# Two rows W·a₁ and W·a₂ for a graph-attention layer: made on the engines in place of a trip through DRAM

## The chip, the core and the metric

The kernel runs on one core of one Trainium2 chip. A core has five engines with an instruction stream each: PE (matrix products), DVE (vector), ACT (scalar activations), POOL (GpSimd, which here mostly issues indirect transfers) and SP (which here only issues plain transfers). Sixteen DMA engines are shared by all queues of the core. The metric is the device time of one execution in microseconds, as the median of several runs.

## The reference, cut to what matters

Two layers work on x of 32 batches × 512 nodes × 512 features, with a sparse 512×512 adjacency matrix (about four edges for each node).

```python
h = relu(layernorm(x))
x = x + attention(h, adj)          # 8 heads of 64, scores masked by adj, then @ Wo + bo
h = relu(layernorm(x))
g = h @ W                          # layer 1
s1 = g @ a[:512];  s2 = g @ a[512:]
e = leaky_relu(s1[:, None] + s2[None, :], 0.2) * adj
x = x + elu(softmax(e) @ g + beta * g)
```

The sums s1 and s2 need no product h·W first: s1 = h·(W a₁) and s2 = h·(W a₂). So the kernel makes two vectors of 512 numbers once, W a₁ and W a₂, spreads each over all 128 partitions as the tiles `wa1_r` and `wa2_r`, and afterwards needs one dot product for each node and each of the two.

## The kernel before, in words

Each batch is cut into four tiles of 128 nodes. Stage a of a batch normalises x, turns it (transposes on PE), and makes queries, keys and values: queries by four products of 128×512 for each tile, keys and values for two tiles together by seven half products in Strassen's manner (`keys_and_values`, L851). They are written to tables in DRAM. Stage b gathers, tile by tile, the table rows of each edge's two ends (POOL, L959 and L986), multiplies and sums them (DVE, L1037 and L1041), weighs the values (ACT, L1051), adds up edges by products with a 0/1 matrix into `px` (L1017), divides (L1077), turns the result, multiplies by Wo, adds x, normalises again and stores the row hx for layer 1 (`layer0`, L1022). In it the two dot products with `wa2_r` and `wa1_r` stand at L1106 and L1110 (their trace line is L1102). Layer 1 of a batch runs in the stage b of the batch two later (LAG = 2). So batches 0 and 1 come first without any layer-1 work, and their gathers read smaller tables (`tkv`).

The order of the instructions on each engine is written out by a planner when the kernel is built (`Plan.order`, L118). Every operation has an engine, an estimated time, a due time called key, and the buffers it reads and writes. The planner steps through a simulated time and takes on each engine the ready operation with the lowest key. A ready operation with a late key is taken as soon as no other one is ready on its engine. The estimates only decide the order; on the chip each engine runs its list strictly in that order and waits for what an instruction needs. Each key of the main stages is 100 plus 20 for each tile that came before.

Of the start, what the change touches: `constants` (L349) lists small loads on SP with key 20, among them the columns `bq_c` and `bk_c`. These hold the two biases with one word for each partition and column, which are only read in `general_path`, the branch taken for inputs that the fast path can't treat. `dot_rows` (L690) makes the two rows. For g = 0 and 1: SP loads a₁ or a₂ to all partitions (L695), DVE multiplies it with the four 128-row blocks of W and sums (L699, four times), which leaves W·a as a 128×4 tile `wa[g]`; SP writes those 512 words to a DRAM row in the right order (L702), and when that has landed reads the row back to all partitions (L705). The keys are KD and KD + 10 with KD = 110.

The products with the matrix of ones that the change uses exist already in `edges` (L377): `turn` (L421) multiplies a diagonal matrix by a column, and a product with `onesP` adds over partitions, so that a column becomes a row on all partitions. PSUM banks for such results come from the ring `D` (six banks, taken in the order in which operations need one); the ring `w` has four 128×512 tiles.

Of the kernel before, what the change touches and what calls it, by code (L numbers as in the profile page):

```python
# [9 lines left out]
F32 = mybir.dt.float32  # L10
I32 = mybir.dt.int32
AF = mybir.ActivationFunctionType
ALU = mybir.AluOpType
# [6 lines left out]
P = 128  # L20
# [19 lines left out]
def product(nc, out, lhsT, rhs, start=True, stop=True):  # L40

    nc.tensor.matmul(out, lhsT, rhs, start=start, stop=stop)  # L42


def bcast_rows(ap, n):

    return bass.AP(tensor=ap.tensor, offset=ap.offset, ap=[[0, P], [1, n]])
# [17 lines left out]
class Plan:  # L65
# [14 lines left out]
    def buf(self, tag, name=""):  # L80
        return Buf(tag, name)

    def op(self, eng, us, key, fn, r=(), w=(), dma=0, form=128):
        def parts(xs):
            return [x if isinstance(x, tuple) else (x, None) for x in xs]

        r, w = parts(r), parts(w)
        o = Op(eng, us * self.PACE.get(eng, 1.0), key, fn, r, w, [], dma)
        o.form = form
        evict = eng in ("DVE", "ACT") and any(b.tag in self.free_order for b, _ in r + w)  # L90
        o.rank = key - self.FREE * evict
        for xs, write in ((r, False), (w, True)):
            for b, part in xs:
                for other, opart, owrite in b.log:
                    if (write or owrite) and other is not o and (
                        part is None or opart is None or part == opart
                    ):
                        o.before[other] = True
                b.log.append((o, part, write))
        for b in dict.fromkeys(b for b, _ in r + w):  # L100
            b.users += 1
            if b.first is None and b.tag in self.rings:
                b.first = o
                o.alloc.append(b)
            elif b.first is not None and b.first is not o:
                o.behind[b.first] = True
        self.ops.append(o)
        return o
# [110 lines left out]
def kernel(  # L219
# [23 lines left out]
    nc = tc.nc  # L243
    B, N, D = x.shape
    T = N // P
    C = D // P
# [4 lines left out]
    def ctile(shape, name, dt=F32):  # L251
        return const.tile(shape, dt, name=name, tag=name)
# [3 lines left out]
    ident = ctile([P, P], "ident")  # L256
    bq_c, bk_c = ctile([P, C], "bq_c"), ctile([P, C], "bk_c")
    beta_b = ctile([P, 1], "beta_b")
    flag = ctile([1, 1], "flag", I32)
# [4 lines left out]
    dram = fast.enter_context(tc.tile_pool(name="dram", bufs=1, space=bass.MemoryType.DRAM))  # L264

    def wtile(shape, name, dt=F32):
        return work.tile(shape, dt, name=name, tag=name)

    def ring(n, shape, name):
        return [wtile(shape, f"{name}{i}") for i in range(n)]  # L270
# [23 lines left out]
        "dn": ring(3, [P, 3, T], "dn"),  # L294
        "s1": ring(3, [P, T], "s1"),
        "cs": ring(LAG + 1, [P, C], "cs"),
        "row": [dram.tile([N], F32, name=f"row{i}", tag=f"row{i}") for i in range(2)],
        "tab": [dram.tile([N + DUMMY, ROW], F32, name=f"tab{i}", tag=f"tab{i}") for i in range(LAG + 2)],
        "tkv": [dram.tile([N + DUMMY, HO], F32, name=f"tkv{i}", tag=f"tkv{i}") for i in range(LAG)],
        "th": [dram.tile([N + DUMMY, HW_], F32, name=f"th{i}", tag=f"th{i}") for i in range(LAG)],  # L300
# [5 lines left out]
    buf, op = plan.buf, plan.op  # L306

    wt2, wt3, wt4 = (wtile([P, C // 2, D], n) for n in ("wt2", "wt3", "wt4"))
    one32, onesP = wtile([P, G], "one32"), wtile([P, P], "onesP")
    bq_r, bk_r, c_row = (wtile([P, D], n) for n in ("bq_r", "bk_r", "c_row"))  # L310
    wa1_r, wa2_r = wtile([P, D], "wa1_r"), wtile([P, D], "wa2_r")
# [3 lines left out]
    perm, posi = wtile([P, T], "perm", I32), wtile([P, T], "posi", I32)  # L315
    fin = wtile([P, T, 2], "fin")
    rmax = wtile([P, T, H], "rmax")
    dmax = wtile([P, 2, T], "dmax")
    bad = wtile([P, T], "bad")
    cap = wtile([P, 2, T], "cap")  # L320
# [4 lines left out]

    C_ = {n: buf(None, n) for n in (
        "wq", "wk", "wv", "wo", "w1", "rows", "c_row", "wa", "OH", "nzE", "idx", "qidx", "fin",
        "rmax", "dmax", "bad", "cap", "flag", "perm", "posi", "t1", "t2", "t3", "t4",
    )}

    def setup():
# [16 lines left out]

    def constants():  # L349

        def load(fn, dma=4096, w=()):
            op("SP", 0.1, 20.0, fn, w=w, dma=dma)

        for dst, src in ((bk_r, bk), (bq_r, bq)):
            load(lambda dst=dst, src=src: nc.sync.dma_start(dst, bcast_rows(src, D)), P * D * 4, [C_["rows"]])
        load(lambda: nc.sync.dma_start(beta_b, bcast_rows(beta, 1)))
        zero = rings["qe"][-1].rearrange("p a b -> p (a b)")
        for tag, n in (("tkv", D), ("qtab", QW), ("th", HW_), ("tab", ROW)):
            for tab in rings[tag]:
                for c0, c1 in ((0, D), (HO, ROW)) if tag == "tab" else ((0, n),):  # L360
                    m = 1 if tag == "qtab" else DUMMY
                    load(lambda tab=tab, c0=c0, c1=c1, m=m: nc.sync.dma_start(
                        tab[N:, c0:c1], zero[:m, : c1 - c0]))
        for dst, src in ((bq_c, bq), (bk_c, bk)):
            load(lambda dst=dst, src=src: nc.sync.dma_start(
                dst, bass.AP(tensor=src.tensor, offset=src.offset, ap=[[1, P], [P, C]]),
                allow_slow_non_contiguous=True))

# [313 lines left out]
        op("DVE", 0.7, 30.0, lambda: nc.vector.scalar_tensor_tensor(  # L684
            c_row, c_row, -1.0, p.ap, op0=ALU.add, op1=ALU.add), r=[p], w=[C_["c_row"]])

    KD = 110.0
    GL, ZL = 0.5, 0.2

    def dot_rows():  # L690
        wa = buf("s1", "wa"), buf("s1", "wa")
        for g in range(2):
            ar, scr, row = buf("w", "ar"), buf("w", "scr"), buf("row", "wrow")
            k = KD + 10 * g
            op("SP", 0.1, k, lambda g=g, ar=ar: nc.sync.dma_start(  # L695
                ar.ap, bass.AP(tensor=a.tensor, offset=a.offset + g * D, ap=[[0, P], [1, D]])),
               w=[ar], dma=P * D * 4)
            for c in range(C):
                op("DVE", 0.8, k, lambda g=g, c=c, ar=ar, scr=scr: nc.vector.tensor_tensor_reduce(  # L699
                    scr.ap, w1[:, c, :], ar.ap, 1.0, 0.0, op0=ALU.mult, op1=ALU.add,  # L700
                    accum_out=wa[g].ap[:, c : c + 1]), r=[C_["w1"], ar], w=[scr, wa[g]])
            op("SP", 0.1, k, lambda g=g, row=row: nc.sync.dma_start(  # L702
                row.ap.rearrange("(t p) -> p t", p=P), wa[g].ap, allow_slow_non_contiguous=True),
               r=[wa[g]], w=[row], dma=2048)
            op("SP", 0.1, k, lambda g=g, row=row: nc.sync.dma_start(  # L705
                (wa1_r, wa2_r)[g], row.ap.unsqueeze(0).to_broadcast([P, N])),
               r=[row], w=[(C_["wa"], g)], dma=P * D * 4)

# [572 lines left out]

    load_weights()
    constants()
    edges()
    stage_a(0)
    right_sums()
    value_row()
    dot_rows()  # L1290
    for b in range(B + LAG):
        if b + 1 < B:
# [213 lines left out]
```

## Time and profile before

| what | value |
|---|---|
| median of 3 runs | 2711.84 us (2710.35 to 2716.46) |
| the profiled execution | 2710.42 us, with a span of 2708.6 us in the trace |
| PE busy | 2652.9 us |
| DVE, ACT, POOL busy | 2058.6, 1925.6 and 1830.4 us |
| DMA | 789.56 MB, 291 GB/s over the span |
| packets under 512 B | 34627 of 237154 |

The page divides the span into 40 slices and gives for each the busy share of the engines, the clock granted to PE, the share of the DMA engines and the rate. A second kind of view gives the same for stretches that one names. The views of waits say how long an engine stood still and which event ended it. The timeline lists instructions of one engine in order of time with the idle time before them in brackets.

### The profile page before, as it was taken

Reading aid. Unit: us, or ns where it says so; the run is one execution under the profiler, and the core shown is the slowest. Engines: PE = TensorE matmul, PEld = TensorE weight load, DVE = VectorE, ACT = ScalarE, POOL = GpSimd, SP = SyncE. Lnnn points to the kernel's source line nnn. Section 1 sums busy time; section 2 is a strip of 40 time slices with the busy share of each in tenths; the row PEclk is TensorE's granted clock in tenths of the full one; section 3 lists DMA queues with packets and bytes.
Section 4 is the critical chain, followed back from the end, with each engine's and each line's share of the span. In section 5 each row is a group of like instructions: output and inputs, shape, how many; then the busy total and the mean of one; then the engine's idle time right before and its main releaser. Section 6 shows DMA issues by size and latency. Waiting matters only on the chain. (4 is left out here: it accounts for less than half of the span.)

```text
span 2708.6 us, 39840 instructions
## 1 busy us (share of the span) xinstructions
PE 2652.9 (98%) x10262; PEld 1215.4 (45%) x10262; DVE 2058.6 (76%) x5241; ACT 1925.6 (71%) x6181; POOL 1830.4 (68%) x1710
## 2 busy tenths in 40 slices
PE   9999999999999999999999999999999999999987
PEld 4434444444444444444444444444444444444433
DVE  7767777777877777777777777777777777777675
ACT  1557777687777777777777777777777777777672
POOL 2776766666766766766766766766766766766664
PEclk9999999999999999999999999999999999999999
DMA  5988888888888888888888888988888988988984
GB/s 181 261 283 318 302 304 300 288 303 309 302 297 302 300 297 311 294 290 313 300 303 304 304 290 301 313 300 300 309 291 300 311 299 296 314 294 288 304 260 123
DMA packets 237154, 789.56 MB, mean 291 GB/s; under 512 B 34627, under 2 KB 34627, under 8 KB 236918
## 3 DMA queue, kind: packets, MB, share of 16 engines
q0 software_dynamic: 156736, 644.99, 70.6%
q1 hardware_dynamic: 80182, 141.95, 14.1%
q8 instruction: 83, 1.36, 0.2%
q14 instruction: 153, 1.25, 0.1%
HBM read 617.36 MB, written 169.46 MB: 290 GB/s over the span
## 5 line engine op out<-in xcount | busy, mean ns | idle before, releaser
L1051 ACT ACTIVATE kv<-kv 128x64 f32<-128x64 f32 x4096 | 1012.0, 336 | 5.2
L986 POOL DMA_INDIRECT qe<-qtab,qidx x504 | 550.3, 1092 | 218.9 <-issue 111.0
L959 POOL DMA_INDIRECT kv<-tab,idx x480 | 509.4, 1061 | 164.9 <-issue 112.3
L42 PE MATMUL pd<-wq,hT 128*128 128x512 f32 x1024 | 465.2, 597 | 1.4 <-ACT hT L795 1.4
L42 PE MATMUL pd<-wo,oT 128*128 128x512 f32 x1032 | 464.4, 593 | 0.1
L42 PE MATMUL pd<-w,gT 128*128 128x512 f32 x992 | 447.8, 594 | 0.0
L773 POOL DMA_INDIRECT x<-in_x_dram,perm x252 | 356.2, 1414 | 85.3 <-issue 51.0
L1037 DVE TENSOR_TENSOR qe<-qe,kv 128x1024 f32<-128x1024 f32 x252 | 307.2, 1220 | 39.2 <-DMA qe<-qtab,qidx 30.7
L1041 DVE TENSOR_REDUCE s<-qe 128x16 f32<-128x1024 f32 x252 | 305.7, 1214 | 0.1
L42 PEld LDWEIGHTS pd<-wq,hT 128*128 128x128 f32 x1024 | 195.3, 192 | 244.1 <-issue 241.5
L42 PEld LDWEIGHTS pd<-wo,oT 128*128 128x128 f32 x1032 | 194.7, 190 | 239.5 <-issue 220.3
L42 PEld LDWEIGHTS pd<-w,gT 128*128 128x128 f32 x992 | 188.4, 191 | 239.3 <-issue 230.8
L760 POOL TENSOR_TENSOR mv<-mv,mhalf 128x1 f32<-128x1 f32 x256 | 170.4, 666 | 170.0 <-DVE mv L757 152.7
L778 POOL DMA_INDIRECT out_dram<-w,perm x128 | 157.7, 1232 | 158.6 <-DVE w L1253 113.6
L871 PE MATMUL pd<-wt,S 128*128 128x512 f32 x496 | 238.1, 602 | 3.8 <-DVE k L879 3.7
L871 PE MATMUL pd<-wk,hT 128*128 128x512 f32 x496 | 237.9, 603 | 3.7 <-ACT hT L795 3.4
L871 PE MATMUL pd<-wv,S 128*128 128x512 f32 x496 | 233.6, 593 | 4.0 <-DVE S L860 2.1
L1247 ACT ACTIVATE w<-pd,dn 128x512 f32<-128x512 f32 x128 | 87.7, 685 | 194.6 <-PE pd L42 194.5
L1094 DVE TENSOR_TENSOR x<-pd,x 128x512 f32<-128x512 f32 x128 | 88.0, 687 | 127.8 <-PE pd L42 113.1
L1102 DVE CUSTOM_DVE_ANT_0 w<-hx,wa_r 128x512 f32<-128x512 f32 x256 | 175.2, 684 | 12.0 <-ACT hx L767 11.5
L755 DVE BATCH_NORM_STATS2 st<-x 128x6 f32<-128x512 f32 x256 | 176.3, 689 | 3.5 <-DMA x<-in_x_dram 0.9
L740 PEld LDWEIGHTS pd<-ident,w 128*128 128x128 f32 x1152 | 133.1, 141 | 82.2 <-issue 37.4
(217 smaller groups left out, 3590.1 us busy)
## 6 DMA issues: line engine op xcount, KB each, us to landing
qtab<-q SPq DMA_DIRECT2D x124, 258.0 KB
tab<-hx SPq DMA_DIRECT2D x120, 260.0 KB
tab<-v SPq DMA_DIRECT2D x120, 260.0 KB
tab<-k SPq DMA_DIRECT2D x120, 256.0 KB
qe<-qtab,qidx POOLq DMA_INDIRECT x504, 6.6
kv<-tab,idx POOLq DMA_INDIRECT x480, 8.0
x<-in_x_dram,perm POOLq DMA_INDIRECT x252, 7.6
th<-hx SPq DMA_DIRECT2D x8, 260.0 KB
```

Of the source, the lines that this page charges most:

```text
L42: nc.tensor.matmul(out, lhsT, rhs, start=start, stop=stop)
L755: nc.vector.bn_stats(s6.ap, src.ap)
L760: op("POOL", 0.75, key, lambda: nc.gpsimd.tensor_tensor(mv.ap[:, t, 2:3], mv.ap[:, t, 2:3], mhalf[:, 0:1], op=ALU.pow), w=[(mv, t)])
L773: nc.gpsimd.indirect_dma_start(dst, None, rows, bass.IndirectOffsetOnAxis(ap=perm[:, t : t + 1], axis=0), **lim)
L778: nc.gpsimd.indirect_dma_start(rows, bass.IndirectOffsetOnAxis(ap=perm[:, t : t + 1], axis=0), src, None, **lim)
L871: nc.tensor.matmul(p.ap, lhs()[:, c, :], rhs[:, c, :], start=first and c == 0, stop=c == K2 - 1, skip_group_check=True)
L959: nc.gpsimd.indirect_dma_start(dst, None, tab.ap, bass.IndirectOffsetOnAxis(ap=idx[:, t, g : g + 1], axis=0), bounds_check=N + DUMMY - 1, ...
L986: op("POOL", 1.3, kb - 0.84 * S + 0.1 * g, lambda qs=qs, g=g, t=t: nc.gpsimd.indirect_dma_start(q_row(qs, g), None, s["qtab"].ap, bass.Ind ...
L1037: nc.vector.tensor_tensor(q, q, sl.ap[:, at, KO : KO + D], op=ALU.mult)
L1041: nc.vector.tensor_reduce(sb.ap[:, at, :], q.rearrange("p n (h f) -> p n h f", f=HD), axis=AX.X, op=ALU.add)
L1051: nc.scalar.activation(p[:, h, 0:HD], p[:, h, 0:HD], AF.Copy, scale=p[:, h, HD : HD + 1])
L1102: nc.vector.tensor_tensor_reduce(scr.ap, hx.ap[:, 1 : D + 1], row, 1.0, 0.0, op0=ALU.mult, op1=ALU.add, accum_out=dst)
```

## The change

The two rows no longer pass through DRAM. DVE multiplies a diagonal matrix of 128×(4·128) by the column tile `wa[g]`, PE multiplies the result by the matrix of ones into a bank of the ring `D`, and ACT copies the bank to `wa1_r` or `wa2_r`. The two DRAM buffers fall away. KD goes from 110 to 100, so the eight multiply-and-sum operations get earlier keys too. The loads of `bq_c` and `bk_c` get the key 1500 in place of 20, and a mark `late` as the thing they write, which makes them follow one another.

```diff
@@ rings @@
-        "row": [dram.tile([N], F32, name=f"row{i}", tag=f"row{i}") for i in range(2)],
@@ constants @@
-        def load(fn, dma=4096, w=()):
-            op("SP", 0.1, 20.0, fn, w=w, dma=dma)
+        def load(fn, dma=4096, w=(), key=20.0):
+            op("SP", 0.1, key, fn, w=w, dma=dma)
...
         for dst, src in ((bq_c, bq), (bk_c, bk)):
             load(lambda dst=dst, src=src: nc.sync.dma_start(
                 dst, bass.AP(tensor=src.tensor, offset=src.offset, ap=[[1, P], [P, C]]),
-                allow_slow_non_contiguous=True))
+                allow_slow_non_contiguous=True), key=1500.0, w=[C_["late"]])
@@ dot_rows @@
-    KD = 110.0
+    KD = 100.0
...
-            ar, scr, row = buf("w", "ar"), buf("w", "scr"), buf("row", "wrow")
+            ar, scr, p = buf("w", "ar"), buf("w", "scr"), buf("D", "pwa")
...
-            op("SP", 0.1, k, lambda g=g, row=row: nc.sync.dma_start(
-                row.ap.rearrange("(t p) -> p t", p=P), wa[g].ap, allow_slow_non_contiguous=True),
-               r=[wa[g]], w=[row], dma=2048)
-            op("SP", 0.1, k, lambda g=g, row=row: nc.sync.dma_start(
-                (wa1_r, wa2_r)[g], row.ap.unsqueeze(0).to_broadcast([P, N])),
-               r=[row], w=[(C_["wa"], g)], dma=P * D * 4)
+            op("DVE", 0.7, k, lambda g=g, scr=scr: nc.vector.tensor_tensor(
+                scr.ap.rearrange("p (c q) -> p c q", c=C), ident.unsqueeze(1).to_broadcast([P, C, P]),
+                wa[g].ap.unsqueeze(2).to_broadcast([P, C, P]), op=ALU.mult), r=[wa[g]], w=[scr])
+            op("PE", 0.86, k, lambda scr=scr, p=p: product(nc, p.ap, onesP, scr.ap), r=[scr], w=[p])
+            op("ACT", 0.6, k, lambda g=g, p=p: nc.scalar.copy((wa1_r, wa2_r)[g], p.ap), r=[p], w=[(C_["wa"], g)])
```

More of the change, by code (lines that the diff above doesn't have):

```diff
@@ L327 @@
         "wq", "wk", "wv", "wo", "w1", "rows", "c_row", "wa", "OH", "nzE", "idx", "qidx", "fin",
-        "rmax", "dmax", "bad", "cap", "flag", "perm", "posi", "t1", "t2", "t3", "t4",
+        "rmax", "dmax", "bad", "cap", "flag", "perm", "posi", "late", "t1", "t2", "t3", "t4",
     )}
```

## The prediction

> **What bounds the kernel now.** I read the page's first lines, then busy time by stretches of 100 us, then PE's waits, then the start in steps of 2 us, then single instructions of SP, POOL and PE.
>
> ```profile
> span 2708.6 us, 39840 instructions
> PE 2652.9 (98%) x10262; PEld 1215.4 (45%) x10262; DVE 2058.6 (76%) x5241; ACT 1925.6 (71%) x6181; POOL 1830.4 (68%) x1710
> ```
>
> PE is the bound: only 2708.6 - 2652.9 = 55.7 us of the span are without a product. So a change is worth what it does to these 55.7 us, plus products added or removed. Where they lie (columns: stretch, length, busy us of PE, its weight loads, DVE, ACT, POOL; clock granted; DMA share; rate):
>
> ```profile
> 100.00:200.00 100.00, 90.66 (x313) 39.91 (x312) 67.52 (x142) 58.53 (x199) 73.97 (x68) 0.98 0.93 278
> 200.00:300.00 100.00, 95.69 (x379) 42.82 (x378) 76.30 (x179) 72.37 (x242) 68.46 (x64) 0.98 0.84 291
> 500.00:600.00 100.00, 97.13 (x397) 44.59 (x396) 74.50 (x192) 78.72 (x260) 65.07 (x62) 1.00 0.85 295
> 900.00:1000.00 100.00, 100.00 (x370) 46.32 (x369) 77.93 (x200) 77.11 (x253) 73.85 (x68) 1.00 0.91 316
> 2600.00:2700.00 100.00, 86.98 (x362) 38.09 (x362) 65.93 (x219) 51.52 (x141) 54.50 (x53) 0.91 0.56 166
> ```
>
> The first 100 us lose 5.8, the next two hundred 9.3 and 4.3, single waits up to 900 us about 7, then nothing up to 2500, and the end loses 30. PE's waits from 100 to 240 us (us in total, times, longest):
>
> ```profile
> PE pd L871 <- DVE k L879: 3.4, 1, 3.4
> PE pd L740 <- DVE w L1077: 3.3, 2, 3.1
> PE pd L871 <- DVE S L860: 2.1, 1, 2.1
> PE pd L740 <- ACT x L767: 1.4, 1, 1.4
> PE pd L931 <- DVE mv L762: 1.3, 1, 1.3
> ```
>
> With two smaller ones it is 13.2 us. Beside it, in the windows of 2 us, stands the trace of the word-by-word writes: DMA engines busy, hardly a byte moved.
>
> ```profile
> 96.00:98.00 2.00, 2.00 (x6) 0.95 (x5) 1.21 (x4) 2.00 (x9) 1.67 (x3) 1.00 0.96 335
> 102.00:104.00 2.00, 2.00 (x6) 0.76 (x4) 2.00 (x6) 1.83 (x8) 1.66 (x2) 1.00 0.57 61
> 122.00:124.00 2.00, 0.63 (x4) 0.00 (x1) 1.90 (x6) 2.00 (x8) 1.57 (x1) 1.00 0.59 48
> ```
>
> The chain behind it, from the timelines of SP, POOL and PE: the row is written at 96.90 and read back at 108.43, after its landing; likewise 110.60 and 129.41. POOL stands still for late transfers, its square roots (L760) come late, DVE stops behind them, and PE behind DVE.
>
> ```profile
> 96.90 0.37 SPq L702 DMA_DIRECT2D row<-s  x1
> 108.43 0.32 SPq L705 DMA_DIRECT2D wa_r<-row  x1
> 129.41 0.32 SPq L705 DMA_DIRECT2D wa_r<-row  x1
> 125.81 1.01 POOL L986 DMA_INDIRECT qe<-qtab,qidx  x1 [2.03 <-DMA kv<-tkv,idx]
> 132.72 1.00 POOL L959 DMA_INDIRECT kv<-tkv,idx  x1 [1.13 <-DMA x<-in_x_dram,perm]
> 144.01 1.09 POOL L760 TENSOR_TENSOR mv<-mv,mhalf 128x1 f32<-128x1 f32 x2
> 146.10 3.45 PE L871 MATMUL pd<-wt,S 128*128 128x512 f32 x4 [3.38 <-DVE k L879]
> 221.15 0.76 PE L740 MATMUL pd<-ident,w 128*128 128x128 f32 x4 [3.06 <-DVE w L1077]
> ```
>
> In the instruction order each POOL transfer waits for the landing of the one eight transfers before it; so slow DMA becomes POOL waits. POOL has little to give: from 80 to 180 us it is busy 16 of every 20 us and loses 0.3 us at nearly each issue, except for 4.9 us of waits between 123.8 and 132.7.
>
> **What the change removes.** Two writes of 512 words, two reads of 256 KB, four SP issues. From 90 to 98 us DMA moves 326 GB/s on average; from 100 to 108 it moves 113 and from 120 to 124 it moves 44. That is 5.2 and 3.5 us of transfer time lost, 8.7 in all. SP's wait of 7.5 us (two) before L705 goes too; queued behind it were a key store and the mean rows of `tkv` (L942 at 129.82), which batch 1's first gather at 149.11 reads with some 19 us to spare: nothing gained there.
>
> A rule of the Trainium skill speaks against a gain: "DMA: Bandwidth & Descriptors", section "Anatomy of one DMA — SWDGE (gpsimd) path", prices a transfer at a nearly constant 2.0 us plus its bytes at 436 GB/s. By it (stated for POOL's path) write and read-back cost 2.0 and 2.6 us, all hidden since the first reader of `wa_r` starts at 141.06, and the sum would be a loss of the added products alone. The trace has 11.5 us from first write to read-back and 18.8 for the second, and the low rates above. I go by the trace.
>
> **What it adds.** PE: two products of 128x512 with ones; the same product at 25.97 is followed by the next at 26.83, so 2 x 0.86 = 1.7 us, on the bound, counted in full. DVE: two diagonals, at 0.69 for the same operation (L423); ACT: two bank copies at 0.59 (L1092's row). From 100 to 120 us these engines are busy 13.2 and 10.2 of 20; were that cover gone, it would be 1.4 and 1.2 us. Each product also holds one of the six banks until ACT's copy. No row shows what that costs: from 0 (below it nothing, since a held bank frees no one) to the 3.4 of the nearest wait of this kind, at 146, where a bank waited for L879; I take 0, because both products stand where PE had no wait before.
>
> New waits: PE's products wait for DVE's diagonals, with a `px` group and half products queued behind. By the walk below the diagonals are ready near 96 and 105, and PE arrives at 102.5 and 106: no stall. ACT waits for each product, with a relu of x and the weighing of `kv` tile 96 behind it; they are done near 104.5 and 113.6, and PE wants them at 116 and 118: covered, with some 5 us to spare.
>
> **What it moves.** The bias columns are not moved far back. In the new order the load of `bq_c` stands where it stood and that of `bk_c` two places later, behind the fourth x tile and `bq_r`: the planner takes a ready operation when its engine has nothing else. All of it is at 27 to 31 us, where PE has 20.00 of 20 us. Worth 0; were PE not covered by queued products, the x tile could gain about the 2 us that one such load holds the queue.
>
> The dots come earlier: four of them and the diagonal now stand before the second half of tile 0's score sum, so ACT's weighing of `kv` starts some 2 us later. PE needed it at 104.33 and had it by 98.0: covered. POOL's next two query gathers then move behind one x fetch and two `kv` gathers, 4 to 5 us later. Walking the new order with the old durations (1.3 us for a gather with its issue gap, 1.87 for an adding fetch, 0.75 for a root), the next `px` group is reached and ready near 118.5 on both sides. Then the mean product still waits for roots behind 17 us of POOL transfers: 2.0 us in place of 1.26 + 1.37, a gain of 0.6. The pair of roots of 144.01 has the same transfers before it, less 4.9 us of waits, so near 139: the stall of 3.38 goes, and with it the slow clock after it (3.45 for 1.88 and 0.87 for 0.60: 1.8), together 5.2. The 2.09 at 164 hung on a later root of the same chain: gone. The 3.06 at 221 with 1.7 of slow clock (5.23 for 3.60) comes from a `kv` slot that PE freed at 202.8 and a gather behind it; such a slot wait can return: half, 2.4.
>
> Here the second rule: "TensorE: Matmul & The Clock Gate", "What's actually happening", lets the clock fall after an idle window of about 3.4 us. The trace has it fall to 0.57 over 4 us after 3.06 too, and not after 1.87 (552.59). By the page neither stall is quite long enough, and my sum would be 1.8 + 0.8 = 2.6 us smaller; I use the trace.
>
> The start so gains 5.2 + 2.1 + 2.4 + 0.6 = 10.3 us.
>
> Against it stands the run-in. Both orders are the same from about PE row 3064 of 6330 to the end, so the end's 30 us stay. But the old order repeats itself from the column sums at 1005.77; the new one only six batches later, at the place that runs at 1491.19 before. In the old run-in PE waited 7.1 us from 240 to 900, 0.87 a batch; six more batches cost 0 to 5.2. A count in the orders: a `px` group with at most 1.0 us of PE work before the turn of its quotient (L740 behind L1077) occurs 5 times before and 10 times after; three of the five waited, 2.1 us together, so 0.42 each and 2.1 more. I take 2.5.
>
> **Sum.** The profiled execution took 2710.42 us (span and 1.8 around it): 2710.42 - 10.3 + 1.7 + 2.5 = 2704.3. The median is 1.4 above that execution: 2705.7.
>
> **The rivals.** *Given back.* The start gains half (5), since POOL stays full from 80 to 180 us whatever DMA does, and the run-in costs its 3 to 5: 2711.84 - 5 + 1.7 + 3.5 = 2712. For it: POOL's rate. Against: its waits there name DMA.
>
> *Slower, by the run-in.* Six more batches of an unsettled order, with one stall over 3 us and its clock: 5.2 + 3.1 + 1.7 = 10.0, plus 1.7 for products, less a start that gains only 3: 2711.84 + 8.7 = 2720.5. It decides once run-in waits pass 10.3 - 1.7 = 8.6 us at the full gain. For it: the doubled short handovers. Against: after 240 us no old wait passed 2 us.
>
> *The change is hidden*: rows were not needed before 141, so only the products count: 2713.5. The rates speak against it; I put it with the second case. That the bias part does nothing holds in all.
>
> **How the numbers follow.** A run of this kernel can be told from no change at about 0.2%, 5.4 us. The gain at the start outlasting the run-in has 0.42, given back or hidden 0.33, slower 0.25. The range goes from 2698 (221 gone too, no run-in cost, the old waits of the run-in partly gone) to 2722, the slower case with a little more.
>
> **What would show it.** Right: no rate under 100 GB/s from 96 to 126 us, POOL's waits for transfers there gone, PE's waits from 100 to 240 down from 13.2 to about 5, and those from 240 to 1500 near 10. Wrong: the same PE waits in that first stretch, a new stall over 3 us with a clock of 0.57 behind it, or products slower than 0.86.

## The result and the profile after

The changed kernel takes 2707.7 us (median of 22 runs, 2699.6 to 2711.5) where the kernel before, on the same chip, takes 2711.5 us (22 runs). The ratio is 0.9983 with a 95% interval of 0.9977 to 0.9989, so 3 to 6 us less. On a second chip it was 0.9974 (0.9964 to 0.9984). The prediction was 2705.7.

The profiled execution took 2708.17 us. Its first lines on the page:

```profile
span 2706.4 us, 39822 instructions
PE 2658.8 (98%) x10266; PEld 1217.8 (45%) x10266; DVE 2058.1 (76%) x5243; ACT 1923.9 (71%) x6183; POOL 1814.7 (67%) x1710
```

Without a product are now 2706.4 - 2658.8 = 47.6 us, 8.1 less than before; but PE is busy 5.9 us longer. Of that, 1.7 are the new products. The rest is clock: this execution ran at a mean granted clock of 0.991, the one of before at 0.993, and from 0 to 100 us, where PE's order is nearly the same in both, at 0.93 in place of 0.97. That early part is not the change's: executions of its order gave 0.93 to 0.97 there (0.97 in `pool_less`), and the order of before 0.93 in `no_write` and 0.98 in `old_order`.

By stretches of 100 us (start, end, length, busy us of PE, its weight loads, DVE, ACT, POOL; clock; DMA share; rate):

```profile
100.00:200.00 100.00, 93.15 (x336) 40.61 (x335) 72.12 (x151) 64.81 (x225) 76.40 (x70) 0.97 0.87 274
200.00:300.00 100.00, 99.70 (x373) 45.82 (x372) 78.81 (x191) 74.89 (x255) 70.12 (x69) 1.00 0.91 322
500.00:600.00 100.00, 99.74 (x405) 45.86 (x405) 78.18 (x196) 72.66 (x237) 67.54 (x63) 1.00 0.85 291
1300.00:1400.00 100.00, 97.27 (x353) 44.28 (x352) 75.01 (x186) 72.99 (x243) 67.12 (x63) 0.98 0.88 304
```

The two stretches from 100 to 300 gain 2.5 and 4.0 us, and 500 to 600 gains 2.6. New is a loss of 2.7 at 1300 to 1400, where PE was full before. PE's waits from 100 to 240 us (total, times, longest):

```profile
PE pd L870 <- DVE k L878: 3.5, 2, 3.2
PE pd L870 <- DVE v L878: 1.4, 1, 1.4
PE pd L930 <- DVE v L878: 1.4, 1, 1.4
PE pd L739 <- DVE w L1076: 0.9, 1, 0.9
```

That is 7.2 us in place of 13.2. (Line numbers after the edit are lower by one.) The mark of the word writes is gone; these are windows of 2 us, and 108 to 110 is the lowest between 96 and 126:

```profile
102.00:104.00 2.00, 2.00 (x6) 0.85 (x5) 1.41 (x5) 1.19 (x5) 1.66 (x2) 1.00 0.96 332
108.00:110.00 2.00, 2.00 (x6) 0.75 (x6) 2.00 (x4) 0.58 (x1) 1.70 (x2) 1.00 0.77 117
122.00:124.00 2.00, 2.00 (x12) 0.68 (x4) 0.00 (x0) 0.00 (x0) 1.69 (x2) 1.00 1.06 267
```

POOL no longer stands still for a transfer: from 88 to 178 us it has no wait over 0.31. Yet the roots that DVE needs hardly come earlier, as its timeline shows (start, duration):

```profile
124.05 1.61 POOL L759 TENSOR_TENSOR mv<-mv,mhalf 128x1 f32<-128x1 f32 x3
142.79 1.10 POOL L759 TENSOR_TENSOR mv<-mv,mhalf 128x1 f32<-128x1 f32 x2
```

And PE's timeline has the two new products without a wait before them, and the old stall near 146 almost unchanged, slow clock included (3.78 for 1.88 and 4.63 for 3.60):

```profile
103.61 1.02 PE L42 MATMUL pd<-w,onesP 128*128 128x512 f32 x2
107.40 1.02 PE L42 MATMUL pd<-w,onesP 128*128 128x512 f32 x2
...
145.81 3.78 PE L870 MATMUL pd<-wt,S 128*128 128x512 f32 x4 [3.24 <-DVE k L878]
149.38 4.63 PE L42 MATMUL pd<-wq,hT 128*128 128x512 f32 x8
```

So two things need an explanation. The start gained, but not where the prediction put the gain; and from 240 to 900 us, where the prediction expected a cost, most of the idle time disappeared.

### The profile page after: what moved, and what is told of

Read it like the earlier page. It is cut to its first block, busy times and chain, and to the rows that moved or that the text cites. A ratio compares the mean times of both kernels' runs of the same rounds, so it can differ in the third digit from the quotient of the medians.

```text
span 2706.4 us, 39822 instructions
## 1 busy us (share of the span) xinstructions
PE 2658.8 (98%) x10266; PEld 1217.8 (45%) x10266; DVE 2058.1 (76%) x5243; ACT 1923.9 (71%) x6183; POOL 1814.7 (67%) x1710
## 4 chain that ended last, share of the span: by engine, by line
PE 93%; DMA 2%; DVE 2%; ACT 1%; issue 1%; POOL 1%; SPq 0%; POOLq 0%; DVEq 0%
PE pd L42 49%; PE pd L870 27%; PE pd L739 7%; PE pd L1016 4%; PE px L1016 4%; PE pd L930 1%; PE pd L1123 1%; DMA qe<-qtab,qidx 1%; DMA kv<-tkv,idx 1%; DMA kv<-tab,idx 0%; DMA x<-in_x_dram,perm 0%; ACT kv L1050 0%; DVE w L1252 0%; DVE w L1076 0%; DMA x<-in_adj_dram 0%
## 5 line engine op out<-in xcount | busy, mean ns | idle before, releaser
L985 POOL DMA_INDIRECT qe<-qtab,qidx x504 | 535.6, 1063 | 233.1 <-issue 111.0
L777 POOL DMA_INDIRECT out_dram<-w,perm x128 | 151.0, 1179 | 163.1 <-DVE w L1252 111.8
```

The source lines that it names most:

```text
L985: op("POOL", 1.3, kb - 0.84 * S + 0.1 * g, lambda qs=qs, g=g, t=t: nc.gpsimd.indirect_dma_start(q_row(qs, g), None, s["qtab"].ap, bass.Ind ...
```

## The experiments

They ran on four chips. On one, called the slower chip below, the kernel before takes 2729.3 us (`no_write`, `trip_back`, `kd110` and `products_twice`), on the others 2711.0, 2712.7 and 2712.8; so times are compared as ratios to it. 0.001 is 2.7 us.

### Is it the word writes?

`no_write` is the kernel before, in its own order, without the two word writes; the wide rows are then read from `a` itself, so the dots of this kernel are taken with a and not with W a.

```diff
-            op("SP", 0.1, k, lambda g=g, row=row: nc.sync.dma_start(row..., wa[g].ap, ...),
+            op("SP", 0.1, k, lambda: None,
                r=[wa[g]], w=[row], dma=2048)
-                (wa1_r, wa2_r)[g], row.ap.unsqueeze(0).to_broadcast([P, N])),
+                (wa1_r, wa2_r)[g], bass.AP(tensor=a.tensor, offset=a.offset + g * D, ap=[[0, P], [1, D]])),
```

> The kernel before, in its own order, with the two word-by-word writes left out; the two rows are read from a itself and not from W times a, so the output differs, but the timing of everything else is the same. Theory 1 (slow transfers set the start): PE's waits from 100 to 240 us fall by half and the time falls by 4 to 8 us against before. Theory 2 (POOL's own issuing sets the start, and the gain of the change came from another order of instructions): at most 1 us less than before, and POOL's root pair near 144 us comes at most 1.5 us earlier.

Measured: 2722.52, ratio 0.9973 (0.9961 to 0.9985), 7.4 us less. The windows in which the old trace moved 113 and 44 GB/s now move (this kernel's stretches, same columns):

```profile
100.00:108.00 8.00, 8.00 (x34) 3.33 (x32) 6.29 (x12) 4.68 (x19) 6.71 (x6) 1.00 0.95 284
120.00:124.00 4.00, 3.27 (x28) 1.00 (x26) 0.84 (x3) 2.33 (x10) 3.18 (x5) 1.00 1.04 330
```

POOL has no wait over 0.31 us from 110 to 140 there. But its pair of roots comes at 142.71, and PE waits 13.8 us from 100 to 240, no less than the old trace on the first chip: the fall by half that the first theory expected did not come. The kernel before was not profiled on this chip, but PE's list is the same, so one can count from a product that both traces have, here before and then `no_write`:

```profile
88.24 1.98 PE L871 MATMUL pd<-wt,hT 128*128 128x512 f32 x4 [0.24 <-ACT v L895]
```

```profile
91.18 1.98 PE L870 MATMUL pd<-wt,hT 128*128 128x512 f32 x4 [0.24 <-ACT v L894]
144.80 1.98 PE L870 MATMUL pd<-wt,S 128*128 128x512 f32 x4 [2.82 <-DVE k L878]
```

From it to the product behind the stall (146.10 before) it is 57.9 us before and 53.6 here, both at a granted clock of 1.00. So 4.2 us were gained by then, by arriving earlier and not by waiting less at that stall. Where the rest of the 7.4 was gained the traces do not show.

`trip_back` is the changed kernel with the two word writes put back for nobody: DVE's diagonal is followed by the write of `wa[g]` to a DRAM row that is never read.

```diff
+            def diagonal(g=g, scr=scr):
+                nc.vector.tensor_tensor(scr..., ident..., wa[g]..., op=ALU.mult)
+                nc.sync.dma_start(rings["row"][g].rearrange("(t p) -> p t", p=P), wa[g].ap, ...)
```

> The changed kernel in its own order, with the two word-by-word writes of 512 words added where the diagonals are made; nobody reads what they write. Theory 1: 3 to 6 us slower than the changed kernel, so about level with before or slower. Theory 2: within 1 us of the changed kernel (2707 to 2709), with rates under 100 GB/s back for some 10 us.

Measured: 2733.01, ratio 1.0021 (1.0009 to 1.0033). The changed kernel did not run on this chip. The nearest that did is `products_twice` (below), the same order with 1.7 us more products and without the writes: 2730.7. So the writes cost about 4 us (an estimate, 2733.0 - 2730.7 + 1.7, and a rough one: single runs of either spread over 10 us). PE's timeline and POOL's waits (110 to 128 us) in it:

```profile
123.65 3.78 PE L875 MATMUL pd<-wv,S 128*128 128x512 f32 x4 [6.68 <-DVE v L883]
149.78 3.78 PE L875 MATMUL pd<-wt,S 128*128 128x512 f32 x4 [3.79 <-DVE k L883]
```

```profile
POOL x L777 <- DMA x<-in_x_dram,perm: 2.3, 1, 2.3
POOL qe L990 <- DMA x<-in_x_dram,perm: 1.5, 1, 1.5
```

DMA's rate is down again (121 GB/s from 100 to 108 us), POOL waits for its transfers again, and PE has a stall of 6.7 us with half the clock behind it; in `products_twice` the same product waits 1.37 us, and the three roots come at 123.56 in place of 126.98. Two writes of 2 KB that nobody waits for do this. SP's own order is not the reason: the store of queries behind the writes goes out at 105.76, in `products_twice` at 105.58. So the first step of the prediction holds: word writes make POOL's transfers late, and PE with them.

### The key, the order and the arithmetic

`kd110` is the changed kernel with the old key.

```diff
-    KD = 100.0
+    KD = 110.0
```

> The changed kernel with KD at 110 again. Its order repeats itself from the fourth column sums on, not from the sixteenth, but what it repeats is another order than that of both kernels, up to the end. If the length of the run-in costs what the prediction says (about 0.5 to 0.9 us for each batch), it is 5 to 10 us faster than the changed kernel. If the run-in is free and the start's order matters, it lies within 4 us of it, on either side.

Measured: 2766.63, ratio 1.0137 (1.012 to 1.0154): 37 us more than before. Its start is good (PE busy 134.3 of 140 us from 100 to 240). What is bad is all the rest: the planner's order falls into another repeating pattern, up to the end, in which PE is hardly ever idle and still does less. From 1500 to 2500 us it has 3859 product records there, `no_write` on the same chip 3902. The timelines of `kd110` and then of `no_write` show one difference:

```profile
1610.75 0.60 PE L739 MATMUL pd<-ident,w 128*128 128x128 f32 x4
1611.19 1.88 PE L870 MATMUL pd<-wt,hT 128*128 128x512 f32 x4
1612.91 0.60 PE L739 MATMUL pd<-ident,w 128*128 128x128 f32 x4
```

```profile
1600.68 1.88 PE L870 MATMUL pd<-wt,S 128*128 128x512 f32 x4
1602.40 1.04 PE L739 MATMUL pd<-ident,w 128*128 128x128 f32 x8
1603.27 1.88 PE L870 MATMUL pd<-wv,S 128*128 128x512 f32 x4
```

Turns stand alone between wide products in place of in pairs, and over the whole execution they are busy 236.2 us in place of 226.3. The two profiled spans are 42.8 us apart; such differences, added up over all groups of PE, come to about 25 of them, and 9 are idle time. The rest, and which operation tipped the pattern, stay open.

On the next chip the changed kernel itself ran too, as a yardstick.

> The changed kernel as it is, so that the other kernels of this set stand beside it on one chip. Both theories: 0.998 of the time before (0.9977 to 0.9989 was measured on the first chip).

Measured: 2704.45, ratio 0.9974 (0.9964 to 0.9984).

`b100` is the kernel before with the new key alone.

```diff
-    KD = 110.0
+    KD = 100.0
```

> Before with the key 100 in place of 110 and nothing else: the trip through DRAM stays, the order moves (on PE it repeats itself from batch 12; before from 10, the changed kernel from 16). Theory 1 (the trip is what costs, the order is worth little): within 3 us of before. Theory 2 (the earlier key's order makes the gain): 3 to 7 us less. A third way: an order that settles late costs in its run-in, so 2 to 4 us more.

Measured: 2704.72, ratio 0.998 (0.997 to 0.9989): 5.4 us less with the trip through DRAM still there. Its interval overlaps that of the whole change. It was the second theory's figure, and I had not expected it.

`old_order` is the opposite: the order of before with the change's arithmetic laid in by hand after planning. The diagonal goes into the row tile itself, directly behind the fourth multiplication; the product and ACT's copy go to a place where a bank of `D` is free.

```diff
+                if c == C - 1:
+                    nc.vector.tensor_tensor((wa1_r, wa2_r)[g]..., ident..., wa[g]..., op=ALU.mult)
...
+            op("SP", 0.1, k, lambda: None, r=[wa[g]], w=[row], dma=2048)
+            rows_at.append(op("SP", 0.1, k, lambda: None, r=[row], w=[(C_["wa"], g)], dma=P * D * 4))
...
+            for g, slot in extra.get(i, ()):
+                bank, wide = rings["D"][slot], (wa1_r, wa2_r)[g]
+                product(nc, bank, onesP, wide)
+                nc.scalar.copy(wide, bank)
             o.fn()
```

> The order of before (key 110, all the old operations where the planner had put them) with the change's arithmetic laid in by hand: the diagonal is written into the row tile itself behind the fourth multiplication, the product with ones and ACT's copy stand at two places in the order where a bank is free, near 110 and 129 us. No words go through DRAM. Theory 1 (the word writes cost the start about 7 us whatever the order, and the two products cost about 1.7 on the bound): about 5.5 us less than before, ratio 0.998. Theory 2 (most of the gain comes from the new order): no gain, 0 to 1.7 us more than before. If it is faster than the changed kernel, the new order gave something back.

Measured: 2708.78, ratio 0.9989 (0.9979 to 1.0): 3 us less (0 to 6), between the two expectations. `b100_inlay` is the same with the key 100 (`old_order` with `KD = 100.0`).

> The order of the kernel before with the key 100, and in it the change's arithmetic laid in by hand as in old_order, so that no words go through DRAM. With b100 (0.998 of before) it shows what the trip costs in the new key's order. If the trip costs a fixed amount (7 us by no_write, less 1.7 us for the products): 5 us less than b100, ratio 0.996. If the new key's order had already put the trip where it costs little: the ratio stays within 0.997 to 0.9985, like the changed kernel's 0.9974, and the two parts of the change do not add up.

Measured: 2697.48 (6 runs), ratio 0.9945 (0.993 to 0.996): 15 us less than before, and the fastest of all. PE's waits from 100 to 240 us in it:

```profile
PE pd L744 <- DVE w L1081: 1.5, 1, 1.5
PE pd L43 <- ACT oT L1096: 1.4, 1, 1.4
PE pd L875 <- ACT v L899: 1.1, 1, 1.1
```

No wait there passes 1.54 us, and the clock from 100 to 240 us is 1.00. In `b100` a half product stands for 5.9 us with half the clock behind it, and in `b100_inlay` the same product has no wait (first `b100`, then `b100_inlay`):

```profile
126.72 3.78 PE L871 MATMUL pd<-wv,S 128*128 128x512 f32 x4 [5.86 <-DVE v L879]
```

```profile
122.30 1.88 PE L875 MATMUL pd<-wv,S 128*128 128x512 f32 x4
```

It is the product that waits 6.68 us in `trip_back`, whose key is 100 too. So in this order the trip costs more than in the old one (`b100` to `b100_inlay`: 0.0035, 9.5 us; before to `old_order`: 3 us, both with the products paid), and the two parts don't add up. How much more is not well measured: by `no_write` the writes alone cost 7.4 us in the old order, on another chip.

The idle time of PE by stretch (length less busy time of each stretch) shows which part does what:

| kernel | 100 to 240 | 240 to 900 | 900 to 1500 |
|---|---|---|---|
| before | 13.2 | 7.3 | 0.0 |
| changed, profiled first | 7.2 | 2.3 | 3.6 |
| changed (`after_here`) | 8.1 | 2.1 | 2.4 |
| `old_order` | 10.9 | 7.0 | 0.0 |
| `b100` | 9.9 | 2.6 | 2.2 |
| `b100_inlay` | 5.0 | 2.6 | 2.2 |
| `no_write`, slower chip | 13.8 | 11.3 | 0.0 |
| `trip_back`, slower chip | 11.6 | 5.0 | 5.0 |
| `products_twice`, slower chip | 8.5 | 6.4 | 5.4 |

Within one chip the two right columns hang on the order that the key makes, with or without the trip: key 110 has all these waits before 900 us, key 100 a part of them behind. The exception is `kd110`, in which the planner placed the new operations with the old key (7.4 and 3.3). The left column hangs on both parts. On the slower chip the two right columns together are about as large with either key (11.3 against 10.1 and 11.8), so what the key gains there on the other chips is not shown for it.

### What holds the start: POOL

`pool_plus` gives POOL more to do: two extra roots into a spare tile ahead of each of batch 0's adding fetches of x.

```diff
+        def add_x():
+            if b == 0:
+                for _ in range(2):
+                    nc.gpsimd.tensor_tensor(spare, onesP[:, 0:1], mhalf[:, 0:1], op=ALU.pow)
+            fetch(x1.ap, b, t, ALU.add)
```

> The changed kernel with POOL's work made longer by some 4.6 us in four steps (two extra one-column square roots into a spare tile ahead of each of batch 0's four adding fetches of x); the order is the same on all other engines. Theory A (with the slow writes gone POOL's own pace sets when the roots come, so that the wait of 3.2 us at 145.8 stays): the wait there and the one near 119 grow by some 4 us together and the time by 3 to 6 us against the changed kernel. Theory B (late transfers or another engine set it): POOL's spare time takes the extra work, the time grows by less than 1.5 us.

Measured: 2710.45, ratio 0.9997 (0.9988 to 1.0007), 6.0 us more than `after_here` beside it, for 4.6 us of work. The largest wait, in PE's timeline, is not where I had put it:

```profile
128.14 1.92 PE L931 MATMUL pd<-v,one 128*32 128x512 f32 x4 [5.01 <-DVE v L879]
```

`pool_less` is the counterpart: batch 0's four adding fetches are left out, so x is missing from that batch's attention result.

```diff
-        op("POOL", 1.3, k, lambda: fetch(x1.ap, b, t, ALU.add), ...)
+        op("POOL", 1.3, k, lambda: b and fetch(x1.ap, b, t, ALU.add), ...)
```

> The counterpart of pool_plus: the changed kernel without batch 0's four adding fetches of x (x is not added to the attention result in that batch, so its output differs from the reference's); all orders are otherwise the same. It takes 4 x 1.87 = 7.5 us out of POOL's work before the three roots that ran at 124.2 us. Theory A (POOL's pace sets the start: extra work of 4.6 us cost 6 us, and moving roots only moved the wait to the gathers behind them): the three roots come near 119, as soon as their inputs are there, the waits of PE at 119 to 129 shrink and that of 3.2 us at 146 goes with its slow clock: 5 to 9 us less than the changed kernel, ratio 0.994 to 0.9955 of before. Theory B (POOL is only one of several that are late by then, PE's turn, ACT's copies and DVE's share the delay): 1 to 3 us less, ratio 0.9963 to 0.997.

Measured: 2700.14 (6 runs), ratio 0.9958 (0.9942 to 0.9974), 4 to 7 us less than the changed kernel by the ratios, between the two expectations. The stall of 3.24 us is down to 0.24, as POOL's pace would have it. The run takes 1 MB of transfers out as well; that POOL's time counts without them is what `pool_plus` shows, which adds no transfer.

```profile
136.56 1.98 PE L870 MATMUL pd<-wt,S 128*128 128x512 f32 x4 [0.24 <-DVE k L878]
157.45 0.94 PE L739 MATMUL pd<-ident,w 128*128 128x128 f32 x4 [2.24 <-DVE w L1076]
```

`roots_early` asks whether it is only the roots' place. After planning, in POOL's list alone, the three roots and the two are put ahead of the three transfers before them.

```diff
-    todo = plan.order()
+    todo = ahead(plan.order(), roots)
...
+def ahead(todo, roots):
+    for r in sorted(roots, key=lambda o: o.start):
+        if not ROOTS[0] < r.start < ROOTS[1]:
+            continue
+        for _ in range(NPAST):            # 3
+            ...
+            todo.insert(i, todo.pop(j))   # j: the POOL transfer before root i
```

> The changed kernel with five of POOL's square roots (the three that ran at 124.2 us and the two at 142.97) put ahead of the three transfers that stand before them in POOL's order (an adding fetch of x and two query gathers); all other engines keep their order. Their inputs were ready 5.5 and 5.3 us before they ran. Theory A (roots queued behind POOL's transfers hold the start, whatever the DRAM trip does): the roots run near 120 and 139, the PE wait of 3.2 us at 146 and its slow clock (2.9 us more) go, those of 1.4, 1.4 and 0.9 at 119 to 129 shrink by 1 to 2: 5 to 8 us less than the changed kernel, so 0.9945 to 0.9955 of before. Theory B (another thing is late next, such as the three transfers that now come 1.1 to 1.6 us later): less than 2 us of it stays, 0.997.

Measured: 2705.43, ratio 0.9974 (0.9965 to 0.9984), the same as the changed kernel. The roots did come earlier (118.35 and 136.88; counted from the fourth root, at 87.54, by 4.5 and 4.7 us). The wait moved: DVE now stands for the second query gather, which POOL issued behind the roots, and PE behind DVE (DVE's timeline, then PE's):

```profile
147.35 1.23 DVE L1039 TENSOR_TENSOR qe<-qe,kv 128x1024 f32<-128x1024 f32 x1 [4.46 <-DMA qe<-qtab,qidx]
```

```profile
153.02 3.78 PE L43 MATMUL pd<-wo,oT 128*128 128x512 f32 x4 [4.68 <-ACT oT L1094]
```

Whatever POOL does later, something is late. With the other engines in this order, the amount of POOL's work from about 80 to 150 us, more than the place of its roots, sets when the start is done.

### The remaining terms

`products_twice` issues each of the two products twice.

```diff
-            op("PE", 0.86, k, lambda scr=scr, p=p: product(nc, p.ap, onesP, scr.ap), r=[scr], w=[p])
+            op("PE", 0.86, k, lambda scr=scr, p=p: [product(nc, p.ap, onesP, scr.ap) for _ in range(2)], r=[scr], w=[p])
```

> The changed kernel with each of the two products with ones issued twice into the same bank. If PE's time is counted in full at that place: 1.7 us slower than the changed kernel. If PE's later wait at 142 us for POOL's roots swallows it: 0 to 0.5 us, and that wait is shorter by 1.7 us.

Measured: 2730.7, ratio 1.0009 (0.9999 to 1.0018). In its trace each place takes 1.88 in place of 1.02, so 0.86 a product as counted. The stall at 145.33 behind them is still 3.24, but the wait before the mean product is shorter (0.25, and 1.35 in the changed kernel):

```profile
126.02 1.05 PE L930 MATMUL pd<-v,one 128*32 128x512 f32 x4 [0.25 <-DVE v L878]
```

So 1.1 of the 1.7 us went into that wait. The changed kernel did not run on that chip, and there the stretches after 240 us lose more in all kernels; so the time can't be set against its own. With 1.7 us taken off, the changed kernel would take some 2729.0 us there (an estimate), and before takes 2729.3: that the change gains anything on this slower chip is not shown.

`bias_general` takes the loads of the bias columns out of the start and puts them into `general_path`.

```diff
-        for dst, src in ((bq_c, bq), (bk_c, bk)):
-            load(..., key=1500.0, w=[C_["late"]])
@@ general_path @@
+    for dst, src in ((bq_c, rows[3]), (bk_c, rows[4])):
+        nc.sync.dma_start(dst, ...)
```

> The changed kernel with the two loads of bias columns really taken out of the start and put into the branch that reads them; PE's order is the same. The prediction gave the loads no cost because PE has queued products at 27 to 31 us: no difference from the changed kernel, 0.9974 of before (0.9966 to 0.9982). The rival in the prediction: an x tile comes up to 2 us earlier and the time falls by 1 to 2 us, ratio 0.9967.

Measured: 2706.42, ratio 0.9982 (0.9972 to 0.9992), not to be told from the changed kernel. The loads cost nothing where they were.

## Why the prediction was right, and where it wasn't

The time came out 2 us above the forecast and the sign was right. But two steps were wrong, in opposite directions, and partly cancel, so that the number came out is in part luck. Of the signs that the prediction had set itself, no rate is under 100 GB/s and POOL's waits for transfers are gone; but PE's waits from 100 to 240 us fell to 7.2 and not to 5, and those from 240 to 1500 are 5.9 and not 10.

- **What removes time.** That the word writes slow all DMA and so POOL was right, and it is shown both ways by `no_write` and `trip_back`. The rule of the Trainium skill that was weighed against it ("DMA: Bandwidth & Descriptors", "Anatomy of one DMA — SWDGE (gpsimd) path", a near-constant cost and bytes) would have made the change a loss of its products. It was right to go by the trace's rates.
- **The pair of roots near 139, and 5.2 us from the stall at 146.** This is the step that failed. It moved the roots and left PE's arrival at the stalled product where it had been. POOL's half was nearly right. From the fourth root, up to which POOL's and PE's lists are the same, to the pair it is 54.1 us, against 58.1 before and 53.2 by the walk: 4.0 of the 4.9 us of waits were gained. (1.7 of the 4.9 were a wait for a turn of PE and not for a transfer.) That this root comes at 88.71 in place of 85.90, and so the pair only 1.2 earlier, is the clock of this one execution: from 66 to 73 us it was 0.50, before 1.00, and DVE stood for a product there, first before and then after:

```profile
72.49 0.69 DVE L684 SCALAR_TENSOR_TENSOR c_row<-c_row,pd 128x512 f32<-128x512 f32 x1 [0.47 <-PE pd L42]
```

```profile
75.30 0.69 DVE L683 SCALAR_TENSOR_TENSOR c_row<-c_row,pd 128x512 f32<-128x512 f32 x1 [3.50 <-PE pd L42]
```

  In `products_twice`, with the same list and a clock of 1.00 there, the fourth root follows the second by 13.8 us as before, and not by 16.8. But PE came earlier too. From the product at 91.05 (88.24 before) to its arrival at the stall it is 51.5 us in place of 54.5, because the new order puts eight products of queries behind the stall that stood ahead of it, first before and then after:

```profile
124.49 3.60 PE L42 MATMUL pd<-wq,hT 128*128 128x512 f32 x8
```

```profile
91.05 1.98 PE L870 MATMUL pd<-wt,hT 128*128 128x512 f32 x4 [0.24 <-ACT v L894]
149.38 4.63 PE L42 MATMUL pd<-wq,hT 128*128 128x512 f32 x8
```

  So the roots gained 4.0 us, PE's arrival 3.0, and the stall stayed (3.24, and 2.9 of slow clock behind it; 1.8 in `after_here`). In the old list PE comes earlier too, as its own waits before 142 shrink (50.8 us in `no_write`, 52.0 in `old_order`), and stalls of 2.82 and 2.20 stay.
- **164, 221 and the mean product.** The 2.09 at 164 went, as predicted. The 3.06 at 221 went whole, where half was counted. The mean product's group waits 1.37 + 1.35 + 0.89 in place of 1.26 + 1.37, where 2.0 was predicted: its roots wait for POOL too. Together PE's waits from 100 to 240 fell by 5 to 6 us, and the slow clock behind them by about 1 (3.5 before, 2.9 and 1.8 after), against 10.3 in the sum.
- **The products, 1.7.** Right in size and place, and no wait before them. That they count in full is not shown: of the same amount added once more, 1.1 us went into a wait (`products_twice`). That holding a bank costs 0 was not tested by itself.
- **The longer run-in, +2.5.** Wrong in sign. The order does settle later, but PE's waits from 240 to 1500 went from 7.3 us to 5.9 (4.5 in `after_here`). Six more unsettled batches do bring back 2.4 to 3.6 us, among them one of 2.46 at 1390.86 that costs 1.6 of slow clock more. But the waits from 240 to 900, which the prediction carried over from the old order as a rate for each batch, belong to the order that key 110 makes: `b100` has 2.6 us of them and `old_order` 7.0, on one chip. A wait of one order is no rate for another. Nor did short handovers between `px` and its turn predict anything: doubled in number, they wait less (1.5 us in four from 240 to 1500, where before it was 2.1 in three).
- **The bias columns, 0.** Right, by `bias_general`.
- **Given back.** This rival had named POOL's pace, and that part is true: the start gained half. It erred where the prediction did, in the cost of the run-in.

The sum with what was measured: -5 to -6 for the start's waits, -1 for their clock, +1.7 for products, -1.5 to -3 for the waits from 240 to 1500, and +1.6 clock at 1390 in one of the two profiles: about -4 to -8, where the medians fell by 4 and 7 us on the two chips.

One pair of profiles is a weak measure of the clock, though. Over all runs on the second chip the time lost to it (span times one less the mean granted clock) is 24.5 us on average before (35 runs) and 17.8 with the change (12 runs): 6.7 us apart, where the medians are 6.5 apart. So there fewer slow stretches carry about the whole gain, and the profiled execution of before, at 0.993, was one of those that lost little. In which stretches the other runs lost it is not on record.

What the sum hides too is that the planner, given three new operations and a new key at once, ended 7 to 8 us above what the same operations give when they are laid into the order of `b100`. From `after_here` to `b100_inlay` the profiled spans fall by 6.2 us: 3.1 of idle time from 100 to 240 us, 2.9 of PE's busy time (the clock is 0.95 in place of 0.93 up to 100 us and 1.00 in place of 0.99 to 240), 0.2 elsewhere. Why POOL serves that order better was not traced to a single transfer.

## What to carry to other kernels

A wait carried over from the old trace is only good for the old order: where a planner decides, build the new order, walk the bound engine and the engine that feeds it from the last point that both share, and let both move, since a stall is the difference of two arrivals. When an engine is full over a stretch, moving one of its instructions forward only moves the wait to the ones behind it (`roots_early`); taking work from it is what counts (`pool_less`). And a key that is changed together with an operation deserves a run of its own: here the key alone was worth about as much as the whole change, the old key with the new operations cost 37 us, and operations laid in by hand after planning left the order as it was.

## What the runs showed of the hardware

Two writes of 512 single words each, with nobody waiting for them, held the core's DMA at 121 GB/s from 100 to 108 us (`trip_back`), where it moves 284 without them (`no_write`). They cost 7.4 us in the old order (`no_write`) and about 4, an estimate, in the new (`trip_back`).

The granted clock did not follow the length of a wait. In all 14 traces its slow stretches (0.50) begin on a grid of 3.41 us that is fixed for an execution, and last a whole number of such steps, but for the one that the end cuts off. From 100 to 2400 us, leaving out steps that are slow themselves, one followed each of the 23 steps in which PE was busy for less than 1.4 us, 4 of the 12 with 1.4 to 1.72, and none of the 9366 with more. So what a wait costs hangs on where it falls: 2.24 us within one step of `pool_less` bring half the clock in the next, 2.82 us spread over two steps of `no_write` bring nothing (same columns as the stretches above, first `pool_less`, then `no_write`):

```profile
154.27:157.68 3.41, 1.17 (x5) 0.34 (x4) 1.84 (x6) 0.82 (x1) 3.21 (x4) 1.00 0.99 352
157.68:161.09 3.41, 3.41 (x8) 1.85 (x7) 3.41 (x7) 0.76 (x2) 2.80 (x3) 0.50 0.80 194
```

```profile
139.86:143.28 3.42, 2.12 (x22) 0.84 (x20) 0.59 (x2) 0.28 (x2) 2.78 (x5) 1.00 0.93 163
143.28:146.69 3.41, 1.89 (x5) 0.89 (x6) 3.37 (x10) 1.28 (x2) 2.92 (x4) 1.00 0.68 213
```

The page of the Trainium skill that the prediction weighed ("TensorE: Matmul & The Clock Gate", "What's actually happening") lets the clock fall after an idle window of about 3.4 us. The length agrees with the step; but the step need not be idle, since in `pool_less` 1.17 us of products in it did not keep the clock. Why four of the twelve steps in between were followed by half the clock and eight were not stays open.
